# A graph layer on one core: 26 packed node ranges and 285 row gathers in place of 27 and 263

## The chip, the core and the metric

The kernel runs on one core of one Trainium2 chip. The metric is the device time of one execution in microseconds (us), given as the median of repeated runs. The engines are TensorE (PE; its weight loads are shown as PEld), VectorE (DVE), ScalarE (ACT), GpSimd (POOL) and SyncE (SP). Each engine works through its own queue in the order in which the program was written, so an instruction that waits holds up everything behind it on that engine.

## The reference

There are 6250 nodes with 128 features each and 100000 edges, sorted by their destination. Each edge has a type, 0 or 1, that selects one of two weight matrices. Cut to what matters:

```
Xs  = x[src]
msg = where(edge_type == 0, Xs @ W_data.T + b_data, Xs @ W_control.T + b_control)
agg = segment_sum(msg, dst)                       # 6250 x 128
h   = x + relu(agg + x @ W_self.T + b_self)
out = (h - mean(h)) / sqrt(var(h) + 1e-5)         # per row
```

## The kernel before, in words

**Messages first.** The product of every node with both weight matrices is made once: 12500 possible rows, held on the chip as `m3` (three bf16 parts of each float32 value, so a row has 384 columns) and also written to memory as `table`. This is the lead-in. PE multiplies (L490, L493, L501), ACT and DVE split the result into its parts (L436, L498, L505), and SP issues 13 writes of `table` (L509). After it, summing the messages of a destination is a matter of picking rows and adding them, and the kernel does this in two ways.

**Windows.** The first 27 x 160 = 4320 nodes are handled in 27 ranges of 160 nodes, called windows here. For each window a block of 21 x 128 edges is loaded (`win`). The function `ranks` sorts these edges into slots: it builds one-hot rows (`hots`, L691), counts on PE with triangular matrices how many edges of the same source block came before (L702; the weights are `every`, `tri` and `rest`), takes the count out with a DVE reduction (`slot`, L716), and scatters each edge's source and destination into a small packed list (L752). SP writes that list to memory (`packed`, L772 and L774). The few edges that find no slot are listed as well, and POOL fetches their rows with an indirect transfer (`sr`, L861). `ranks` works on several windows at once: the list `GROUPS` gives 1, 2 and then six times 4 windows. In the first two groups the 21 steps of the count are cut into chains of 6 and 12 steps (`CHAIN`), which run side by side in PSUM; a chain must first be told what the chains before it counted, and `add_to` with `every` does that.

The function `sums` then does one window after another. SP loads the packed list, broadcast to all partitions (`rows`, L904), DVE turns it into one-hot rows (L912), and PE multiplies 98 such blocks with `m3` (stage one, L933, four matmuls of 32 columns at a time). ACT or DVE moves each result out of PSUM (`gs`, L436), and PE multiplies it with a second one-hot matrix (`hot`, made on DVE at L920) into the window's sum `a` (stage two, L947 and L950).

**Gathers.** The last 1930 nodes are handled in blocks of 125 nodes by `gathered`. Per block 17 x 128 edges are loaded, and the last block, with 55 nodes, has 8 x 128. For each 128 edges POOL issues one indirect transfer that fetches 128 rows of `table` (`t_msg`, L1027, 14 buffers), DVE makes a one-hot matrix of destinations for up to six of them at once (`t_hot`, L1021), and PE adds the rows to the block's sum `ga` (L1034; the name has a single PSUM buffer). That makes 15 x 17 + 8 = 263 gathers. Together with the 14 fetches of `sr`, which stand in the same queue, POOL issues 277 such transfers.

`close` finishes windows and gathered blocks: it adds the parts, adds the residual, normalises, and writes `out` (L561 to L616).

**The order of the work.** Nothing is scheduled at run time. The class `Plan` collects all operations with an assumed duration, a due time and their dependencies, and simulates the engines once when the program is built; the order in which it starts operations is the order in which they are written into each engine's queue. A value `slack` on an operation holds it back by that much in the simulation, so that it is placed later in its queue; it adds no wait to the program. For the gathers the planner uses the duration `GC` and spaces their due times evenly:

```
    g0, g1 = T0 + G0, T0 + (NW + G1) * TW
    step = max((g1 - g0) / max(sum(GT), 20), GC + 0.02)
```

With `T0` = 36, `TW` = 13, 27 windows and 263 gathers the step is 1.32 in the planner's own units.

Of the kernel before, what the change touches and what calls it, by code (L numbers as in the profile page):

```python
# [16 lines left out]
SP = mybir.EngineType.SP  # L17
# [4 lines left out]
P = 128  # L22
# [16 lines left out]
WN = 160  # L39
KT = 21  # L40
WIN = KT * P
GROUPS = [1, 2] + [4] * 6
NW = sum(GROUPS)
R = 32
W4 = WN - P
# [46 lines left out]
class Plan:  # L92
# [10 lines left out]
    def add(self, engine, dur, fn, due, r=(), w=(), lat=0.0):  # L103
        alts = engine if isinstance(engine, list) else [(engine, dur, fn)]
        op = Op(alts, due, lat)
        op.index = len(self.ops)
        kind = [(i[0] if isinstance(i, tuple) else i).name for i in w] or ["out"]
        if engine == "SP" and due > self.FROM:
            op.slack = self.SLACK.get(kind[0], 0.0)
        self.ops.append(op)  # L110
        deps = set()
        for items, writes in ((r, False), (w, True)):
            for item in items:
                b, key = item if isinstance(item, tuple) else (item, None)
                for k, (ws, rs) in b.keys.items():
                    if key is None or k is None or k == key:
                        deps.update(ws)
                        if writes:
                            deps.update(rs)
                if writes and key is None:  # L120
                    b.keys = {}
                ws, rs = b.keys.setdefault(key, ([], []))
                if writes:
                    b.keys[key] = ([op], [])
                else:
                    rs.append(op)
                if not b.users or b.users[-1] is not op:
                    b.users.append(op)
        deps.discard(op)
        op.deps = list(deps)  # L130
        return op
# [95 lines left out]
@with_exitstack  # L227
def kernel(ctx, tc, x, xt, edges, w, bias, out):
    nc = tc.nc
    const = ctx.enter_context(tc.tile_pool(name="const", bufs=1))  # L230
    total = const.tile([1, 1], I32, name="total")

    with ExitStack() as main:
        sums_over_windows(main, tc, x, xt, edges, w, bias, out, total)

    matched = nc.values_load(total[0:1, 0:1])
    with tc.If(matched != E), ExitStack() as rest:
        sums_over_all(rest, tc, x, xt, edges, w, bias, out)
# [9 lines left out]
def sums_over_windows(ctx, tc, x, xt, edges, w, bias, out, total):  # L248
    nc = tc.nc
    V, A, G, T, S = nc.vector, nc.scalar, nc.gpsimd, nc.tensor, nc.sync  # L250
# [6 lines left out]
    add = plan.add  # L257

    table = dram.tile([NT * P, D3], BF16, name="table")
    packed = dram.tile([len(GROUPS), 2, P, NT], BF16, name="packed")  # L260

    def B(pool, shape, dtype, name, bufs=1, room=None):
        return Buf(plan, pool, shape, dtype, name, bufs, room)

    def C(shape, dtype, name):
        return Buf(plan, const, shape, dtype, name, 1)
# [3 lines left out]
    TW = 13.0  # L270
    LAT = 0.1
    G0, G1 = 0.0, -4
    GC = 1.3
    SPD = 0.45
    RP, RA, RS = 1, 14, 0.9

# [4 lines left out]
        lat=4.0)  # L281
# [15 lines left out]
    def vec(due, cols, fn, r, w, rate=1.04):  # L297
        return add("DVE", dve(cols, rate), fn, due, r, w)
# [44 lines left out]
    every = C([P, P], BF16, "every")  # L343
# [13 lines left out]
    for i in range(3):  # L357
        vec(0.3, P, lambda i=i: V.memset(one3.t[R * i : R * i + 1, :], 1.0), [], [one3], 0.3)
    counts = C([P, len(GROUPS) + NGB], F32, "counts")
    vec(2, 1, lambda: V.memset(counts.t, 0.0), [], [counts])  # L360
# [9 lines left out]
        op=ALU.is_gt), [r0f, bound_f], [begun])  # L370
    row_ps = low()

    def count_rows():
        for h in range(RH):
# [28 lines left out]
                                    start=True, stop=True), 0.8, [first_f, ident], [first_ps])  # L403
# [44 lines left out]
    packed_b = Buf(plan, None, None, None, "packed_b")  # L448
# [27 lines left out]
    for q in range(NS):  # L476
# [5 lines left out]
        n = 2 * nb * D  # L482
        ts = slice(4 * q, 4 * q + 2 * nb)

        for i, b in enumerate(bs):
            c, k, xk = pieces[b]
# [16 lines left out]
            skip_group_check=True), due + 1.2, [minus, (m3, (q, 0))], [mp])  # L503
# [117 lines left out]
    def ranks(gi, w0, nw, when, step, engines):  # L621
        nh = (nw + 1) // 2
        win = B(work, [P, nw, KT, 3], I32, "win", 2, 4 * KT * 3)
        for i in range(nw):
# [3 lines left out]
        n = nw * KT  # L628
# [19 lines left out]
                                                    op=ALU.arith_shift_right), [win], [cb])  # L648
        vec(when, n, lambda: V.tensor_single_scalar(wr(far), win.t[:, :, :, 2], 0.0,
                                                    op=ALU.not_equal), [win], [far])  # L650
# [5 lines left out]
                                                        op=ALU.bitwise_and), [win], [lo])  # L656
# [9 lines left out]
        L = CHAIN.get(gi, KT)  # L666
        nc_ = -(-KT // L)
# [11 lines left out]
        acc = B(ps, [P, 512], F32, "rk" if gi else "ga", 1)  # L679
# [4 lines left out]
        one = lambda k: hv(piece(k))[:, k - ks[piece(k)]]  # L684
        hkey = lambda k: (hots[piece(k)], (piece(k), (k - ks[piece(k)]) // 2))
        for ci in range(4):
            for k in range(ks[ci], ks[ci + 1], 2):
# [9 lines left out]
                        op=ALU.is_equal), [st1, iota1_b], [hkey(k)], 0.52)  # L697
        wide = nw * NT

        def add_to(c, wt, k, start, stop):  # L700
            for j in range(4):
                T.matmul(acc.t[R * j : R * j + R, c * wide : c * wide + wide],  # L702
                         wt.t[:, R * j : R * j + R], one(k).rearrange("p w c -> p (w c)"),
                         start=start, stop=stop, skip_group_check=True)
        mine = lambda r: [(c, c * L + r) for c in range(nc_) if c * L + r < min(KT, c * L + L)]
        for k in range((nc_ - 1) * L):
            add("PE", (nc_ - 1 - k // L) * wide / 2400, lambda k=k: [
                add_to(c, every, k, k == 0 and c == 1, False) for c in range(k // L + 1, nc_)], when + 1.5,
                [hkey(k), every], [acc])
        for r in range(L):  # L710
            due = when + 2 + step * r
            m = mine(r)
            add("PE", len(m) * wide / 2400, lambda r=r, m=m: [
                add_to(c, tri, k, r == 0 and nc_ == 1, k + 1 in (KT, c * L + L)) for c, k in m], due,
                [tri] + [hkey(k) for _, k in m], [acc])
            vec(due, len(m) * wide, lambda r=r, m=m: V.tensor_reduce(  # L716
                slot.t[:, r:KT:L, :],
                acc.t[:, : len(m) * wide].rearrange("p (k w c) -> p k w c", w=nw, c=NT),
                axis=AX.X, op=ALU.max), [acc], [(slot, r)]).lat = 2 * LAT
            m = [(c, k) for c, k in m if k + 1 < min(KT, c * L + L)]  # L720
            if m:
                add("PE", len(m) * wide / 2400, lambda m=m: [
                    add_to(c, rest, k, False, False) for c, k in m], due,
                    [rest] + [hkey(k) for _, k in m], [acc])
        base, slots = BASE, slot_f
        cs = {6: [0, KT], 12: [0, 12, KT]}.get(L, ks)
        for ci, (k0, k1) in enumerate(zip(cs, cs[1:])):
            dc = when + 3 + step * min(L, k1) + 0.5 * ci * (L < KT)
            m = (k1 - k0) * nw
            c = slice(k0 * nw, k1 * nw)  # L730
# [27 lines left out]
        d2 = when + 3.5 + step * L  # L758
        vs = B(work, [P, nh, NT], BF16, "vs", 1, 2 * NT)
# [10 lines left out]
        def put():  # L770
            if both:
                S.dma_start(packed[gi, :both].rearrange("h p c -> p h c"), vs.t[:, :both])  # L772
            if both < nh:
                S.dma_start(packed[gi, both, :64], vs.t[:64, both])  # L774
        add("SP", SPD, put, d2 + 1, [vs], [(packed_b, gi)], lat=2.0)
        to_d = B(work, [P, nw, NS, 2], BF16, "to_d", 2, 4 * NS * 2)
        for t in range(4):
            nx = NS if t < 2 else NS - 1
# [80 lines left out]
        for pr in range(nh):  # L859
            sr = B(work, [P, D3], BF16, "sr", 2)  # L860
            add("POOL", GC, lambda pr=pr, sr=sr: G.indirect_dma_start(  # L861
                out=sr.t[: room(pr)], out_offset=None, in_=table[:, :],
# [106 lines left out]
    def gathered(bis, when, step):  # L969

        nt, k_ = GT[bis[0]], len(bis)
        n = nt * k_
        gi = len(GROUPS) + bis[0]
        top = GB * max(GT)
# [32 lines left out]
        for j, bi in enumerate(bis):  # L1007
# [6 lines left out]
            for k in range(nt):  # L1014
                at = start + step * k
                kk = j * nt + k
                if k % KB == 0:
# [8 lines left out]
                m = B(work, [P, D3], BF16, "t_msg", 14)  # L1026
                add("POOL", GC, lambda m=m, kk=kk: G.indirect_dma_start(  # L1027
                    out=m.t, out_offset=None, in_=table[:, :],
# [16 lines left out]
    todo = []  # L1045
    for gi, nw in enumerate(GROUPS):
        if gi == 0:
            when, step, engines = 0.0, 0.9, ["SP"]
        elif gi == 1:
            when, step, engines = 8.0, 1.1, ["SP", "ACT"]  # L1050
        else:
            when, step, engines = T0 + w0 * TW - 58, 1.8, ["SP"]
            if gi == 2:
                when, step = 36.0, 1.3
        todo.append((gi, w0, nw, when, step, engines))
        w0 += nw
    placed = [ranks(*a) for a in todo]
    held = []
    for gi, w0, nw, *_ in todo:
# [4 lines left out]
        pairs = [(a, d) for _, a, d, _ in got]  # L1064
        if gi < len(GROUPS) - 1:
            close("", w0 * WN, WN, P, pairs, block, end)
# [3 lines left out]
    g0, g1 = T0 + G0, T0 + (NW + G1) * TW  # L1070
    step = max((g1 - g0) / max(sum(GT), 20), GC + 0.02)
    done = 0
# [154 lines left out]
```

## Time and profile before

| | us |
|---|---|
| median of 14 runs | 481.94 (476.54 to 487.32) |
| the profiled execution's own time | 482.76 |
| its span, from the first to the last instruction | 481.2 |
| PE busy | 443.8 |
| DVE busy | 395.0 |
| ACT busy | 354.3 |
| POOL busy | 301.3 |
| POOL, the 263 gathers of `t_msg` | 283.2, mean 1077 ns each |

The time of an execution is 1.6 us longer than its span, which is what lies around the instructions. Busy time is a share of the whole span: PE with 92% looks like the bound. An engine's queue can nevertheless be full with a lower share, when each of its instructions has a fixed pause before it that isn't counted as busy. A wait that is named in the profile is put down to the semaphore that came last.

### The profile page before, as it was taken

How to read it: one execution, taken by the hardware profiler on the slowest of the kernel's cores; microseconds unless marked ns; L12 is line 12 of the kernel's file. 1: busy time of each engine (PE TensorE's matmuls, PEld its weight loads, DVE VectorE, ACT ScalarE, POOL GpSimd, SP SyncE). 2: the span in 40 equal slices, each digit the busy share in tenths (PEclk: the TensorE clock that was granted, in tenths of full speed). 3: DMA queues.
4: the chain of work that ended last, by engine and by line, in shares of the span. 5: the costliest groups of instructions: out<-in, count | busy, mean ns of one | idle time of the engine just before them, and what ended most of it. 6: DMA issues, size and time to landing. Idle time of an engine off the chain costs nothing.

```text
span 481.2 us, 26926 instructions
## 1 busy us (share of the span) xinstructions
PE 443.8 (92%) x11461; PEld 362.2 (75%) x11461; DVE 395.0 (82%) x1271; ACT 354.3 (74%) x891; POOL 301.3 (63%) x290
## 2 busy tenths in 40 slices
PE   4999968997999889999999999999999999999990
PEld 3666656785888768788787878888889888878970
DVE  6799969998999969999888998888978779654343
ACT  2566764765877857778786788877888778989981
POOL 1100045777877777777777776777777757777700
PEclk9999998999999989999999999999999999999996
DMA  4589985438563546542765336764365524746210
GB/s 147 150 242 346 291 264 152 109 93 244 157 187 85 189 121 202 167 139 72 230 194 168 107 82 201 203 185 106 85 214 191 170 76 110 230 140 186 80 52 20
DMA packets 63117, 76.83 MB, mean 160 GB/s; under 512 B 21000, under 2 KB 52893, under 8 KB 62989
## 3 DMA queue, kind: packets, MB, share of 16 engines
q1 hardware_dynamic: 49147, 47.35, 31.3%
q0 software_dynamic: 13456, 27.42, 20.9%
q8 instruction: 91, 1.49, 1.2%
q10 hardware_dynamic: 386, 0.26, 0.2%
q14 instruction: 37, 0.30, 0.2%
HBM read 60.50 MB, written 13.17 MB: 153 GB/s over the span
## 4 chain that ended last, share of the span: by engine, by line
PE 74%; DVE 10%; DMA 7%; ACT 5%; issue 2%; SPq 0%; ACTq 0%; DVEq 0%
PE g L933 22%; PE a L947 20%; PE rk L702 9%; PE ga L1034 8%; PE a L950 3%; PE vt L752 3%; ACT gs L436 3%; DMA rows<-packed 2%; PE g L493 2%; DVE slot L716 2%; DMA t_msg<-table,t_idx 2%; DVE hot L920 1%; PE a L493 1%; ACT to_d L443 1%; PE a L518 1%
## 5 line engine op out<-in xcount | busy, mean ns | idle before, releaser
L1027 POOL DMA_INDIRECT t_msg<-table,t_idx x263 | 283.2, 1077 | 131.2 <-DVE hots L691 43.9
L436 ACT CAST gs<-g 128x384 bf16<-128x384 f32 x639 | 274.1, 481 | 79.4 <-PE g L933 63.2
L947 PE MATMUL a<-gs,hot 128*32 128x384 bf16 x2592 | 251.2, 331 | 7.9 <-ACT gs L436 5.3
L933 PE MATMUL g<-m,rows 128*32 128x384 bf16 x2646 | 255.6, 330 | 1.8 <-DVE rows L912 1.8
L933 PEld LDWEIGHTS <-rows 128*32 128x32 bf16 x2646 | 168.3, 135 | 13.9 <-DVE rows L912 2.1
L950 PE MATMUL a<-gs,hot 128*32 128x128 bf16 x1944 | 159.6, 220 | 0.4 <-issue 0.4
L947 PEld LDWEIGHTS <-hot 128*32 128x32 bf16 x2700 | 116.0, 95 | 35.2 <-issue 16.1
L1034 PE MATMUL ga<-t_msg,t_hot 128*32 128x384 bf16 x1036 | 102.2, 327 | 2.9 <-DMA t_msg<-table,t_idx 2.9
L716 DVE TENSOR_REDUCE slot<-rk 128x4 f32<-128x392 f32 (+1 forms) x138 | 76.5, 554 | 14.6 <-PE rk L702 9.0
L950 PEld LDWEIGHTS <-hot 128*32 128x32 bf16 x2025 | 81.8, 97 | 4.5 <-issue 0.7
L920 DVE TENSOR_TENSOR hot<-iota_b,to_d 128x1280 bf16<-128x1280 bf16 (+1 forms) x81 | 67.4, 842 | 0.0
L702 PE MATMUL rk<-hots,tri 128*32 128x392 bf16 (+1 forms) x588 | 61.2, 321 | 0.0
L702 PE MATMUL rk<-hots,rest 128*32 128x392 bf16 (+1 forms) x556 | 54.4, 321 | 5.0 <-DVE slot L716 4.8
L1034 PEld LDWEIGHTS <-t_hot 128*32 128x32 bf16 x1036 | 49.5, 97 | 6.9 <-issue 3.3
L912 DVE TENSOR_SCALAR rows<-rows,pid 128x1568 bf16<-128x1568 bf16 x54 | 36.0, 672 | 10.6 <-DMA rows<-packed 10.6
L691 DVE TENSOR_TENSOR hots<-iota_b,st 128x784 bf16<-128x784 bf16 (+1 forms) x83 | 39.2, 489 | 0.4 <-PE vt L752 0.2
L1021 DVE TENSOR_TENSOR t_hot<-iota_b,t_code 128x768 bf16<-128x768 bf16 (+2 forms) x47 | 24.6, 523 | 13.6 <-PE ga L1034 13.5
L702 PEld LDWEIGHTS <-rest 128*32 128x32 bf16 x624 | 24.7, 96 | 14.2 <-issue 11.6
L561 DVE TENSOR_REDUCE s<-a 128x128 f32<-128x384 f32 x27 | 15.0, 556 | 22.4 <-ACT bs L436 11.7
L702 PEld LDWEIGHTS <-tri 128*32 128x32 bf16 x672 | 28.6, 97 | 2.5
L752 PEld LDWEIGHTS <-two 128*64 128x64 bf16 x567 | 14.4, 109 | 8.5 <-DVE two L743 3.4
L861 POOL DMA_INDIRECT sr<-table,at x14 | 14.0, 1001 | 7.6 <-DVE at L849 3.5
(188 smaller groups left out, 528.6 us busy)
## 6 DMA issues: line engine op xcount, KB each, us to landing
rows<-packed SPq DMA_DIRECT2D x27, 784.0 KB
table<-m SPq DMA_DIRECT2D x12, 768.0 KB
t_msg<-table,t_idx POOLq DMA_INDIRECT x263
rows<-in_xt SPq DMA_DIRECT2D x8, 256.0 KB
xc<-in_xt SPq DMA_DIRECT2D x6, 320.0 KB
gl<-sr SPq DMA_DIRECT2D x27, 48.0 KB
xr<-in_x SPq DMA_DIRECT2D x5, 256.0 KB
out<-xr SPq DMA_DIRECT2D x5, 256.0 KB
```

The costliest lines, as they stand in the source:

```text
L436: [("ACT", act(cols), lambda: A.copy(o(), src())), ("DVE", dve(cols), lambda: V.tensor_copy(o(), src()))], None, None, due, r, w, lat)
L691: lambda k=k, kn=kn, ci=ci, hs4=hs4: V.tensor_tensor(hv(ci)[:, k - ks[ci] : k - ks[ci] + kn].rearrange("p k w (c d) -> p (k w) c d", d=2), ...
L702: T.matmul(acc.t[R * j : R * j + R, c * wide : c * wide + wide], wt.t[:, R * j : R * j + R], one(k).rearrange("p w c -> p (w c)"), start=s ...
L716: vec(due, len(m) * wide, lambda r=r, m=m: V.tensor_reduce(slot.t[:, r:KT:L, :], acc.t[:, : len(m) * wide].rearrange("p (k w c) -> p k w c ...
L752: T.matmul(vv()[q : q + 64, i // 2, :], two.t[:, (k - k0) * nw + i].rearrange("p f r -> p (f r)"), one(k)[:, i, :], start=k == 0 and i < 2 ...
L912: add("DVE", dve(half * NT, 0.335), lambda sp=sp, rs=rs: V.tensor_scalar(sp.t[:, rs], sp.t[:, rs], pid1.t, None, op0=ALU.is_equal), due - ...
L920: lambda i=i, hot2=hot2, s4=s4, c0=c0, c1=c1: V.tensor_tensor(hot2.t[:, c0:c1].rearrange("p g (c d) -> p g c d", d=2), iota1_b.t.rearrange ...
L933: T.matmul(gp.t[R * t : R * t + R, :D3], sp.t[:, :, 4 * g + t], m3.t[:, 4 * g + t, :], start=True, stop=True)
L947: T.matmul(a.t[R * j : R * j + R, :D3], hot2.t[:, g, R * j : R * j + R], gs.t, start=g == 0, stop=False, skip_group_check=True)
L950: T.matmul(a.t[R * c : R * c + R, D3:], hot2.t[:, g, P:], gs.t[:, c * D : (c + 1) * D], start=False, stop=last, skip_group_check=True)
L1027: add("POOL", GC, lambda m=m, kk=kk: G.indirect_dma_start(out=m.t, out_offset=None, in_=table[:, :], in_offset=bass.IndirectOffsetOnAxis(a ...
L1034: T.matmul(ga.t[R * i : R * i + R, :D3], hot.t[:, k % KB, R * i : R * i + R], m.t, start=k == 0, stop=False, skip_group_check=True)
```

## The change

Four edits:

- `GROUPS` ends in 3 windows instead of 4, so there are 26 windows. The last 2090 nodes are gathered: 16 blocks of 17 and one of 13, which is 285 gathers.
- `GC`, the planner's duration of a gather, is 1.26 instead of 1.3. The step of the due times becomes 1.28 (before 1.32).
- In `add_to`, one matmul writes the same counts into the places of several chains at once, by a broadcast operand, where there was one matmul for each. This concerns the first group alone, which has four chains: there are 72 matmuls and weight loads in place of 144, with the same number of streamed columns. The second group has two chains, and nothing changes in it.
- The write of `packed` of the second group gets a `slack` of 3.0, which moves it back in SP's queue.

```diff
-GROUPS = [1, 2] + [4] * 6
+GROUPS = [1, 2] + [4] * 5 + [3]
...
-    GC = 1.3
+    GC = 1.26
...
-        def add_to(c, wt, k, start, stop):
+        def add_to(c, wt, k, start, stop, n=1):
             for j in range(4):
-                T.matmul(acc.t[R * j : R * j + R, c * wide : c * wide + wide],
-                         wt.t[:, R * j : R * j + R], one(k).rearrange("p w c -> p (w c)"),
-                         start=start, stop=stop, skip_group_check=True)
+                T.matmul(acc.t[R * j : R * j + R, c * wide : (c + n) * wide].rearrange(
+                    "p (n c) -> p n c", n=n), wt.t[:, R * j : R * j + R],
+                    one(k).rearrange("p w c -> p (w c)")[:, None, :].to_broadcast([P, n, wide]),
+                    start=start, stop=stop, skip_group_check=True)
...
         for k in range((nc_ - 1) * L):
-            add("PE", (nc_ - 1 - k // L) * wide / 2400, lambda k=k: [
-                add_to(c, every, k, k == 0 and c == 1, False) for c in range(k // L + 1, nc_)], when + 1.5,
-                [hkey(k), every], [acc])
+            more = nc_ - 1 - k // L
+            add("PE", max(more * wide / 2400, 0.08), lambda k=k, more=more: add_to(
+                nc_ - more, every, k, k == 0, False, more), when + 1.5, [hkey(k), every], [acc])
...
-        add("SP", SPD, put, d2 + 1, [vs], [(packed_b, gi)], lat=2.0)
+        op = add("SP", SPD, put, d2 + 1, [vs], [(packed_b, gi)], lat=2.0)
+        if gi == 1:
+            op.slack = 3.0
```

As the planner sees the new numbers, every queue is written in a somewhat new order.

## The prediction

> **What bounds the kernel now.** I read the page first, then the gathers' tile, POOL's timeline, the same gathers by windows of time, and last the timelines of the end.
>
> ```profile
> PE 443.8 (92%) x11461; PEld 362.2 (75%) x11461; DVE 395.0 (82%) x1271; ACT 354.3 (74%) x891; POOL 301.3 (63%) x290
> ```
>
> By busy share PE is the bound and POOL has a third of its time free. The tile of the gathers and POOL's timeline say otherwise:
>
> ```profile
> L1027 POOL DMA_INDIRECT t_msg<-table,t_idx x263: 942/949/2419, 66.1 to 457.2; - x132
> ```
>
> ```profile
> 66.06 1.00 POOL L1027 DMA_INDIRECT t_msg<-table,t_idx  x1 [43.92 <-DVE hots L691]
> 67.37 0.97 POOL L1027 DMA_INDIRECT t_msg<-table,t_idx  x1 [0.30 <-issue]
> ...
> 76.66 1.12 POOL L1027 DMA_INDIRECT t_msg<-table,t_idx  x1 [0.30 <-issue]
> 81.23 1.03 POOL L861 DMA_INDIRECT sr<-table,at  x1 [3.46 <-DVE at L849]
> 82.57 0.95 POOL L1027 DMA_INDIRECT t_msg<-table,t_idx  x1 [0.30 <-issue]
> ...
> 288.13 0.94 POOL L1027 DMA_INDIRECT t_msg<-table,t_idx  x1 [0.30 <-PE g L933]
> 292.32 1.09 POOL L1027 DMA_INDIRECT t_msg<-table,t_idx  x1 [3.25 <-PE ga L1034]
> ...
> 390.44 0.94 POOL L1027 DMA_INDIRECT t_msg<-table,t_idx  x1 [0.30 <-PE rk L702]
> 394.87 1.61 POOL L1027 DMA_INDIRECT t_msg<-table,t_idx  x1 [3.49 <-PE ga L1034]
> ...
> 455.95 0.94 POOL L1027 DMA_INDIRECT t_msg<-table,t_idx  x1 [0.30 <-issue]
> 457.20 0.95 POOL L1027 DMA_INDIRECT t_msg<-table,t_idx  x1 [0.30 <-PE g L933]
> ```
>
> Before every gather POOL is idle for 0.30 us, whoever is named as releaser, so this is a fixed pause and no wait: the pitch is at least 0.95 + 0.30 = 1.25 us. From 66.06 to 457.20 POOL does nothing else, and only three pauses exceed 0.7 us: 3.46 for the row numbers `at`, and 3.25 and 3.49 where all 14 `t_msg` buffers were full. POOL's queue is therefore as full as PE's: of 391 us some 11 are free. Between 82.57 and 457.20 there are 266 steps (254 gathers, 12 fetches of `sr`); less 7.5 us of longer pauses that is 367.1 / 266 = 1.380 us each.
>
> ```profile
> 285.00:300.00 15.00, 7.34 (x7) 1.00 0.59 177
> 435.00:450.00 15.00, 11.65 (x12) 1.00 0.46 132
> 450.00:465.00 15.00, 6.32 (x7) 1.00 0.26 72
> ```
>
> These are the gathers alone by stretches (start and end, length, POOL's busy us and count, PE's granted clock, DMA share, GB/s): where DVE has little left (435 to 450: 7.5 of 15 us busy) twelve fit into 15 us, at 0.97 each against the mean of 1.077.
>
> **The change part by part.** *One window less* takes work from PE. Counting stage one in order of time, 98 matmuls to a window, the last windows, which have no `ranks` beside them, start at 432.3, 443.7 and 455.0: 11.4 us each. Earlier ones take 14 to 16, so a window's share of `ranks` is some 3.5. PE loses about 15 us. The window's `sr` fetch stays, since a group of 3 needs two, as a group of 4 does.
>
> *22 more gathers* cost PE little: four concurrent matmuls take 0.16 us in the chain, so 22 x 0.16 = 3.5, and PE alone would gain some 11. On POOL they cost 22 pitches, and there is nothing beside them. The changed order shows where: on PE 21 gathers stand behind the last window's last matmul, where before none did. DVE is nearly idle by then, so I take 1.26 each (450 to 458 shows 1.25, 438 to 457 1.28): 27.7 us. Bounds: 27.5 at the floor, 30.4 at the mean of 1.380.
>
> *The smaller `GC`* packs gathers denser in PE's order: gather 200 comes at window 19.7 (before 20.5), gather 136 at 13.7 (14.2). Their buffers come free earlier. The gather blocked until 394.87 waited for number 204's matmul at 394.1; that now stands at window 20.3, which PE reached at 380.1. So the two waits for buffers go, and a 0.7 at 214 with them: 2.9 + 3.2 + 0.7 = 6.8 us, between 0 and 6.8; I take 6.8, as the margin is 14 us. What is late next is the gather itself: PE then trails POOL by only the landing.
>
> *The merged matmuls* save 72 issues. 96 of the old ones were issued between 10.91 and 11.98, 11 ns each, and the columns streamed stay the same: at most 72 x 11 ns = 0.8 us, at least nothing. I take 0.3.
>
> *The moved write of `packed`.* SP stood at it from 58.80 to 61.40, waiting for `vs`, and the last write of `table` behind it went out at 62.80, though its data was ready at 61.8. Now that write goes first, and the first gather may start about 1.0 us earlier. Behind the moved write wait the `rows` broadcasts of windows 1 and 2, which go out some 2.5 us later.
>
> ```profile
> 70.88 0.63 DVE L912 TENSOR_SCALAR rows<-rows,pid 128x1568 bf16<-128x1568 bf16 x1 [3.23 <-DMA rows<-packed]
> ```
>
> DVE waited here for them, with `at` behind; the new order puts two pieces of `hot`, two of `hots` and two reductions (together 3.4 us) ahead. An earlier first gather only lengthens POOL's 3.46 us before 81.23: what counts is `at`. Rows 2.5 us later, 3.4 us of work moved into the wait and one reduction fewer before `at` give 1.2 us earlier; from 3.4 earlier (no pause left) to 2.5 later (the moved broadcasts alone).
>
> **The sum** for POOL's last gather: 82.57 - 1.2 + 367.1 (266 steps) + 0.6 (small pauses that stay) + 27.7 = 476.8 start, 477.7 end. Then its rows land: before, the completion mark came at 459.8, 1.7 after the last gather's end. PE needs 0.6 for the last matmuls:
>
> ```profile
> 463.93 0.34 PE L1034 MATMUL ga<-t_msg,t_hot 128*32 128x384 bf16 x2
> ...
> 464.32 0.23 PE L521 MATMUL ga<-brows,one 128*32 128x128 bf16 x2
> ```
>
> The block's closing takes from 469.33 to the write at 473.01, 3.7; from the issue of the last write to the span's end it was 5.9:
>
> ```profile
> 469.33 0.54 DVE L561 TENSOR_REDUCE s<-ga 55x128 f32<-55x384 f32 x1
> ```
>
> ```profile
> 473.01 0.31 SPq L612 DMA_DIRECT2D out<-xrg  x1
> ...
> 474.83 0.84 SPq L616 DMA_DIRECT2D out<-xr  x2
> ```
>
> With 0.1 for a hop this is 12.0, and the span 489.7. The profiled execution was 1.6 longer than its span (482.76 against 481.2) and lay 0.8 above the median of 481.94, so I expect 490.5 us, 1.8% slower. PE would have done its windows by about 455 and then follows POOL's pitch.
>
> [...] The granted clock was 0.91 in 60 to 75 us, where PE was busy for 11.2 of 15, and 1.00 nearly everywhere else. [...] Gathers that overlap a `hot` build (L920, a tensor-tensor operation) last 1.18 us in the mean, those that overlap none 1.03. [...]
>
> **The rivals.** *Faster, PE stays the bound.* For it speaks PE's 92% and that the two long waits were POOL's for PE. It needs a shorter pitch: the span equals today's if the last gather ends at 469.2, that is at a mean of (469.2 - 82.6) / 288 = 1.342 us. From 396.78 to 457.20 it was 60.4 / 45 = 1.343, so this is not absurd; but that stretch is in the mean already. If POOL reached window 26's end with all 14 buffers full, 7 gathers of the 21 would be left: 455 + 9 + 1 + 12 = 477, a time near 478.
>
> *No change.* `at` 3.4 earlier and a pitch of 1.36 on the 266 steps: 490.5 - 2.2 - 5.3 = 483.
>
> *Slower still.* The waits for buffers stay, since something else holds PE at those places: 490.5 + 6.8 = 497.3. Against it stands the margin of 14 us at number 204 (6 at 136).
>
> *The edit on the lead-in does nothing.* That is half of my forecast already: the 0.3 us and the earlier start vanish in the wait for `at`.
>
> **How the numbers follow.** The forecast, that POOL's queue ends last with the waits gone, gets 0.74; alone it spans 486 to 495 (`at` 2 each way, tail 1, pitch 0.01 each way). Slower still 0.14, no change 0.06, faster 0.06. The range from 483.5 to 498 takes in the forecast and the slower case. A measurement of this kernel tells 0.5% from no change: faster is below 479.5 (0.06), the same up to 484.4 (0.06), slower above (0.88).
>
> **What would show it.** In the changed profile: about 20 gathers with 0.30 us before each after the last stage-one matmul, PE waiting for `t_msg` there, the last gather near 477 and the last stage-one matmul near 455; no pause over 1 us on POOL after 85 us; `at` near 80. A last gather before 470 would prove the sum of pitches wrong; pauses of 3 us near 290 or 390, the part about the buffers.

## The result: 2.2% slower, and the profile after

| | before | changed |
|---|---|---|
| median, us | 482.58 (47 runs, 476.54 to 487.35) | 492.37 (10 runs, 487.07 to 494.99) |
| span of the profiled execution, us | 481.2 | 492.0 |
| last gather ends | 458.15 | 479.65 |
| last stage-one matmul ends | 467.5 | 457.5 |

The ratio is 1.0225, with a 95% interval from 1.0192 to 1.0258; here and below a ratio compares the fast executions of each kernel alone, those within 1.5% of its fastest, while the medians of all executions differ by 2.0%. PE did its windows 10 us sooner, and the execution ended 10.8 us later. The last matmuls of stage one, in the kernel before and in the changed one:

```profile
467.20 0.34 PE L933 MATMUL g<-m,rows 128*32 128x384 bf16 x2
```

```profile
457.14 0.35 PE L936 MATMUL g<-m,rows 128*32 128x384 bf16 x2
```

In the kernel before, no gather starts behind them; in the changed one 17 do. The page's line of busy times hides this again:

```profile
PE 440.9 (90%) x11178; PEld 356.7 (73%) x11178; DVE 390.3 (79%) x1275; ACT 343.7 (70%) x867; POOL 319.9 (65%) x312
```

PE still leads and POOL has a third of its time free. The tile of the gathers (count, then duration in ns as min/median/max, then first and last start) and POOL's timeline show the queue. `L1030` is the line that was L1027:

```profile
L1030 POOL DMA_INDIRECT t_msg<-table,t_idx x285: 942/947/2032, 68.6 to 478.7; - x143
```

```profile
68.62 1.01 POOL L1030 DMA_INDIRECT t_msg<-table,t_idx  x1 [45.87 <-DMA packed<-vs]
69.93 1.43 POOL L1030 DMA_INDIRECT t_msg<-table,t_idx  x1 [0.30 <-issue]
71.66 1.62 POOL L1030 DMA_INDIRECT t_msg<-table,t_idx  x1 [0.30 <-issue]
...
83.24 0.95 POOL L864 DMA_INDIRECT sr<-table,at  x1 [0.30 <-DVE slot L717]
...
387.09 0.95 POOL L1030 DMA_INDIRECT t_msg<-table,t_idx  x1 [1.44 <-PE rk L702]
389.27 1.13 POOL L1030 DMA_INDIRECT t_msg<-table,t_idx  x1 [1.24 <-PE ga L1037]
...
411.97 1.65 POOL L1030 DMA_INDIRECT t_msg<-table,t_idx  x1 [2.64 <-PE ga L1037]
...
477.45 0.95 POOL L1030 DMA_INDIRECT t_msg<-table,t_idx  x1 [0.30 <-issue]
478.70 0.95 POOL L1030 DMA_INDIRECT t_msg<-table,t_idx  x1 [0.30 <-issue]
```

From 68.62 to 479.65 there is no gap of more than half a microsecond but the three pauses shown, of 1.24 to 2.64 us: POOL is the queue that ends last. The pause of 3.25 us near 290 is gone. Of the one of 3.49 us near 390, two of 1.44 and 1.24 us are left, and the one at 412 is new. The first gather starts 2.56 us later than before, not earlier. The gathers alone by stretches (POOL's busy us and count, then PE's granted clock) end like this:

```profile
435.00:450.00 15.00, 11.65 (x12) 1.00 0.31 86
450.00:465.00 15.00, 11.34 (x13) 0.93 0.37 100
465.00:480.00 15.00, 11.29 (x12) 0.50 0.34 96
```

At the end twelve fit into 15 us, a pitch of 1.25, while PE, which has little left but the gathers' matmuls, is granted a clock of 0.50. In PE's list of waits (total us, times, longest) the gathers' rows went from 2.9 us in one wait to:

```profile
PE ga L1037 <- DMA t_msg<-table,t_idx: 17.4, 16, 3.2
```

The end itself, from the timelines of PE, DVE and SP:

```profile
481.29 0.51 PE L1037 MATMUL ga<-t_msg,t_hot 128*32 128x384 bf16 x3 [0.75 <-DMA t_msg<-table,t_idx]
```

```profile
482.37 0.55 DVE L561 TENSOR_REDUCE s<-ga 90x128 f32<-90x384 f32 x1 [6.53 <-PE ga L521]
```

```profile
485.62 0.34 SPq L612 DMA_DIRECT2D out<-xrg  x1
```

Landing 1.64, PE 1.08, closing 3.25, and 6.40 from the issue of the last write to the end: 12.37 us behind the last gather.

### The profile page after: what moved, and what is told of

Same layout as the page of the kernel before. It is cut to its first block, busy times and chain, and to the rows that moved or that the text cites. A ratio compares the mean times of both kernels' runs of the same rounds, so it can differ in the third digit from the quotient of the medians.

```text
span 492.0 us, 26354 instructions
## 1 busy us (share of the span) xinstructions
PE 440.9 (90%) x11178; PEld 356.7 (73%) x11178; DVE 390.3 (79%) x1275; ACT 343.7 (70%) x867; POOL 319.9 (65%) x312
## 3 DMA queue, kind: packets, MB, share of 16 engines
q0 software_dynamic: 14496, 29.53, 21.9%
## 4 chain that ended last, share of the span: by engine, by line
PE 68%; DMA 13%; DVE 6%; ACT 5%; issue 4%; POOL 1%; POOLq 0%; SPq 0%; ACTq 0%
PE g L936 19%; PE a L950 18%; DMA t_msg<-table,t_idx 9%; PE ga L1037 8%; PE rk L702 8%; PE a L953 3%; PE vt L753 3%; ACT gs L436 2%; PE g L493 2%; ACT to_d L443 1%; POOL t_msg L1030 1%; PE a L493 1%; DMA sr<-table,at 1%; DMA win<-in_edges 1%; PE a L518 1%
## 5 line engine op out<-in xcount | busy, mean ns | idle before, releaser
L1030 POOL DMA_INDIRECT t_msg<-table,t_idx x285 | 300.8, 1055 | 136.8 <-DMA packed<-vs 45.9
L436 ACT CAST gs<-g 128x384 bf16<-128x384 f32 x614 | 263.7, 481 | 75.1 <-PE g L936 56.5
L936 PE MATMUL g<-m,rows 128*32 128x384 bf16 x2548 | 244.1, 328 | 1.7 <-issue 1.7
L950 PE MATMUL a<-gs,hot 128*32 128x384 bf16 x2496 | 240.3, 329 | 5.9 <-ACT gs L436 3.8
L1037 PE MATMUL ga<-t_msg,t_hot 128*32 128x384 bf16 x1127 | 113.6, 335 | 19.3 <-DMA t_msg<-table,t_idx 17.4
L717 DVE TENSOR_REDUCE slot<-rk 128x4 f32<-128x392 f32 (+2 forms) x138 | 74.7, 541 | 25.8 <-PE rk L702 17.4
L923 DVE TENSOR_TENSOR hot<-iota_b,to_d 128x1280 bf16<-128x1280 bf16 (+1 forms) x78 | 65.1, 840 | 0.0
L702 PE MATMUL rk<-hots,tri 128*32 128x392 bf16 (+2 forms) x588 | 58.3, 311 | 0.0
L702 PE MATMUL rk<-hots,rest 128*32 128x392 bf16 (+2 forms) x556 | 54.5, 314 | 2.6 <-DVE slot L717 2.6
L691 DVE TENSOR_TENSOR hots<-iota_b,st 128x784 bf16<-128x784 bf16 (+3 forms) x83 | 38.1, 475 | 0.4 <-PE vt L753 0.4
L561 DVE TENSOR_REDUCE s<-a 128x128 f32<-128x384 f32 x26 | 14.4, 556 | 20.3 <-ACT bs L436 16.7
L753 PE MATMUL vt<-hots,two 128*64 128x98 bf16 x525 | 17.1, 209 | 1.0 <-issue 0.8
```

Of the source, the lines that this page charges most:

```text
L436: [("ACT", act(cols), lambda: A.copy(o(), src())), ("DVE", dve(cols), lambda: V.tensor_copy(o(), src()))], None, None, due, r, w, lat)
L691: lambda k=k, kn=kn, ci=ci, hs4=hs4: V.tensor_tensor(hv(ci)[:, k - ks[ci] : k - ks[ci] + kn].rearrange("p k w (c d) -> p (k w) c d", d=2), ...
L702: T.matmul(acc.t[R * j : R * j + R, c * wide : (c + n) * wide].rearrange("p (n c) -> p n c", n=n), wt.t[:, R * j : R * j + R], one(k).rear ...
L717: vec(due, len(m) * wide, lambda r=r, m=m: V.tensor_reduce(slot.t[:, r:KT:L, :], acc.t[:, : len(m) * wide].rearrange("p (k w c) -> p k w c ...
L753: T.matmul(vv()[q : q + 64, i // 2, :], two.t[:, (k - k0) * nw + i].rearrange("p f r -> p (f r)"), one(k)[:, i, :], start=k == 0 and i < 2 ...
L923: lambda i=i, hot2=hot2, s4=s4, c0=c0, c1=c1: V.tensor_tensor(hot2.t[:, c0:c1].rearrange("p g (c d) -> p g c d", d=2), iota1_b.t.rearrange ...
```

## The experiments

The theory is that POOL's queue of gathers ends last, so that 22 more of them cost their pitch (the time from the start of one to the start of the next). The main rival is the lead-in: the first gather came 2.6 us late, and the small edits or the new order could have made a good part of the loss. Every median below stands beside the median of the kernel before in the same series, from 481.9 to 483.4.

### Taking the last 22 gathers away again

In the changed kernel POOL issues no gather for the last 22 blocks of edges; their matmuls stay and use older rows.

```diff
+                if issued[0] < sum(GT) - 22:
+                    m = B(work, [P, D3], BF16, "t_msg", 14)
...
+                    issued.append(m)
+                else:
+                    m = issued[-1]
+                issued[0] += 1
```

> The changed kernel without its last 22 gathers on POOL: their matmuls stay and use the rows of an earlier gather, so the last 2 blocks' sums are left wrong and only POOL's and the landing's work is taken out. Theory A (POOL's queue sets the end): the last gather ends 22 x 1.25 = 27.5 us earlier than 479.65, near 452; the last stage-one matmul stays near 457.5, the 22 gathers' matmuls add at most 3.5, and closing and last write 9.6, so the span is near 471 and the time 473 within 3. Theory B (PE or the landing of rows sets it): 488 or more.

Measured: 475.71 us, ratio to the kernel before 0.986 (0.978 to 0.994), 16.7 below the changed kernel.

```profile
L1031 POOL DMA_INDIRECT t_msg<-table,t_idx x263: 940/948/2035, 66.9 to 449.0; - x132
```

The last gather ends at 449.9, PE finishes stage one at 456.6 and the last gathered matmul at 462.9, and the span is 473.5. So the gathers were the bound, by 16.7 us over PE. The sums of the last blocks are left wrong by this edit. Of the 27.5 us taken off POOL, the rest is where PE takes over.

### The same 22 taken from the kernel before

The same edit in the kernel with 27 windows.

> The kernel before without its last 22 gathers on POOL, their matmuls kept in the same way (the sums of the last blocks are left wrong). Theory A (at 27 windows PE's windows set the end, and POOL's queue, though full, does not): time 482 within 2, last stage-one matmul near 467. Theory B (POOL sets the end before as well): 476 or less.

Measured: 483.86, ratio 1.0045 (1.0001 to 1.0089).

```profile
L1028 POOL DMA_INDIRECT t_msg<-table,t_idx x241: 942/968/2036, 68.1 to 427.1; - x121
```

The last gather now ends near 428 instead of 458, the last stage-one matmul at 466.7, and nothing is gained. At 27 windows PE's windows set the end, and POOL's queue, though nearly full, has room. The two runs together show a crossing: PE ends last with 27 windows, POOL with 26.

### One window less again

```diff
-GROUPS = [1, 2] + [4] * 5 + [3]
+GROUPS = [1, 2] + [4] * 5 + [2]
```

> The changed kernel with one window less again: GROUPS ends in 2, 25 windows, 306 gathers, 13 fetches of sr instead of 14. Theory A (POOL's queue sets the end, and each further gather costs its pitch): 21 x 1.25 to 1.35 less 1.25 for the fetch, 25 to 27 us on top, time 517 to 520; the last stage-one matmul near 446; the 41 or so gathers behind it at 1.25 each. Theory B (the loss of the change was mostly lead-in and waits, not the count): below 507.

Measured: 518.14, ratio 1.0739 (1.0676 to 1.0802). That is 25.8 us over the changed kernel, for 21 gathers more and one fetch of `sr` less: 1.29 us for each of the 20, or 1.19 by the ends of the last gathers in the two profiles (503.47 and 479.65). The last stage-one matmul ends at 444.5, and 47 transfers start behind it. The price of a window is now the pitch of its gathers, as near as these runs can tell.

### Each edit alone

The window count alone (the first of the four edits):

> The kernel before with 26 windows and 285 gathers alone (GC 1.3, separate matmuls, the write where it was). Theory A (22 more gathers in POOL's queue make the loss): 491 to 496, with the pauses for buffers perhaps still there; 26 windows alone also move the second write of table ahead of window loads on SP, so DVE waits over 1 us for a load of win near 23 us and the first gather starts at 67.5 or later. Theory B (merged matmuls and moved write make a third of the loss): 488 to 489.

Measured: 493.68, ratio 1.029 (1.016 to 1.042): the whole loss, without the other three. The last gather ends at 478.2. DVE did not wait for `win`, against the expectation, and the pauses for buffers near 290 and 390 shrank to 1.5 and 2.0 with GC still at 1.3.

The moved write alone:

> The kernel before with the moved write of packed alone. Theory A (as predicted): the last write of table goes out about 1 us earlier than 62.80, the first gather starts near 65.0, and POOL's wait for at grows or stays, so the time is 482 within 1.5. Theory B (the write of table lands when the writes before it have drained, whenever it is issued): the last write goes out near 61.8 and still lands at 65.2 or later, the first gather starts at 66.0 or later; time 482.6 to 484.

Measured: 483.84, ratio 1.0033 (0.9989 to 1.0076): no effect. In its profile the first gather starts at 65.11, as predicted. One profile does not show that the edit did this, as in the six other kernels with separate matmuls it starts anywhere from 65.96 to 68.22.

GC 1.26 alone:

> The kernel before with GC 1.26 alone. Both theories: the pauses for buffers near 288 and 390 us (2.9 and 3.2) go and the last gather ends 6 to 7 us earlier, near 451.5. Theory A (at 27 windows PE's windows set the end): time 480 to 483. Theory B (POOL already set the end before): 475.8.

Measured: 486.56, ratio 1.0088 (1.0047 to 1.0128), slower than either theory said. The pauses for buffers near 290 and 390 go, others of 1.4 and 3.4 us come at 338 and 414, and the last gather ends at 454.8, but PE waits for rows more often, and its last stage-one matmul ends at 472.5 instead of 467.5. From PE's list of waits:

```profile
PE ga L1034 <- DMA t_msg<-table,t_idx: 5.8, 5, 2.9
```

GC 1.34, the other way:

> The kernel before with GC 1.34 alone (step 1.36, near the measured mean pitch of 1.38). Theory A (a GC below the true pitch puts the gathers' matmuls on PE ahead of their rows, and PE's windows wait behind them; 1.26 cost 0.9%): PE waits less for t_msg than 2.9 us, the windows end earlier than 467.5, time 480 to 483, while the buffers stay full longer and POOL's last gather ends at 460 or later. Theory B (POOL's later gathers become the end): 486 or more.

Measured: 488.61, ratio 1.0116 (1.0071 to 1.0162). PE waits 4.0 us for rows, not less than 2.9, and stage one ends at 469.8. So the theory that a GC below the true pitch is what costs falls: both directions lose about 1% at 27 windows. Theory B had the number right, and its reason in part. The last gathered block now ends behind the windows, at 473.6, but POOL is not late: its last gather ended at 464.1. The block's matmuls wait for `ga`, its one PSUM buffer, which DVE empties at 472.1:

```profile
472.15 1.48 PE L1034 MATMUL ga<-t_msg,t_hot 128*32 128x384 bf16 x16 [0.37 <-DVE s L561]
```

What the two directions share is that every queue is written anew.

The merged matmuls alone, in two series:

> The kernel before with the merged matmuls alone (27 windows, GC 1.3, no moved write). After, the 72 merged matmuls and their neighbours of the first group took from 10.78 to 12.57 us where 144 took from 10.91 to 11.95 before. Theory A (the merging itself is slower, 0.22 us for a group of four with 294 columns against 3 x 0.045): the stretch again lasts about 1.8 us, first gather 0.7 us later than before, time 483.3. Theory B (PE ran at half pace until some moment of the execution that has nothing to do with the edit): the pace doubles at a moment that differs from both runs (10.9 and 12.5 us), after which a merged group of four costs no more than 0.13 us; time 482.6 within 1.

> The kernel before with the merged matmuls alone, again, in more executions (e1_merge had 4, from 480.7 to 490.8, and no verdict). Theory A (merging delays the lead-in through the fetch beside the load of win and PE's windows pass it on): 484 to 486. Theory B (no effect at 27 windows): 482.6 within 1. The fetch of instructions again between 21 and 22 us, with DVE's wait of 1 us or more for win.

Measured: the first gave four executions from 480.72 to 490.77, too few and too far apart for a ratio; the second 487.66 in 12 executions, ratio 1.0101 (1.0059 to 1.0143), more than both theories. The first window starts at 57.2 instead of 55.5, so the lead-in is longer; but the kernels are level at window 12 (256.7 and 257.3), and the last 5 us are lost between windows 14 and 24 (437.1 against 432.3 at window 24), where the order of the queues differs. What does it there was not separated.

### Why the lead-in got longer

DVE waits 1.39 us for the load of `win` in the changed kernel. The first suspect was SP's order: with 26 windows the second write of `table` stands ahead of two of these loads. One hold puts it back:

```diff
+            if q == 3:
+                op.slack = 1.5
```

> The changed kernel with one hold of 1.5 on the second write of table, so that SP issues the loads of win before it, as in the kernel before. Theory A (the lead-in's delay passes to the end through POOL's full queue): DVE's wait of 1.4 us for win near 23 us goes, the first gather starts near 67.2 and the last ends 1.4 us earlier, time near 491. Theory B (the later waits take the gain back): 492.4 within 0.7.

Measured: 490.68, ratio to the kernel before 1.015 (1.007 to 1.023); DVE's wait of 1.4 us stays. The order is not the cause, and the 1.7 us against the changed kernel lie within the spread of its executions.

The profiles gave another suspect, the fetch of instructions. The changed kernel with separate matmuls tests it:

> The changed kernel with the separate matmuls of before. In the profiles so far the four kernels with merged matmuls have an instruction fetch of 16 KB between 21.1 and 21.9 us, beside the load of win that is under way, and DVE waits 1.0 to 1.4 us for that load; the six with separate matmuls have the fetch at 22.7 to 24.7 and no such wait. Theory A (the merged form moves the fetch into the load): here the fetch is at 22.5 or later and DVE waits less than 0.3 us, while the time stays 492.4 within 1.5, since POOL's later steps differ more than this. Theory B (the wait comes from SP's order with 26 windows): the wait of 1 us or more is there again.

Measured: 493.69, ratio 1.0241 (1.0179 to 1.0303), and no wait for `win`. DVE's timeline of the changed kernel first, then of this one:

```profile
24.61 0.21 DVE L639 TENSOR_TENSOR rel<-win,wbase 128x42 f32<-128x42 int32 x1 [1.39 <-DMA win<-in_edges]
```

```profile
23.26 0.20 DVE L639 TENSOR_TENSOR rel<-win,wbase 128x42 f32<-128x42 int32 x1
```

In all seven kernels with merged matmuls a 16 KB packet of the instruction queue starts between 20.8 and 21.9 us, while the 252-byte packets of the load of `win` that ACT issued are under way; their last one starts at 23.4 to 24.0, and DVE waits 1.0 to 1.7 us. In the seven with separate matmuls the packet comes at 22.7 to 24.7, and the load's last packet had started by 22.7. With 72 matmuls and as many weight loads fewer in the queue, the fetch comes earlier and meets the load. That the fetch holds the load up is read from these times; no run moved the fetch alone.

This kernel also says what an earlier start is worth. Its tenth transfer starts at 78.95, 4.3 us before that of the changed kernel, yet its last gather ends at 479.95, 0.3 us later. Most of it goes at the first fetch of `sr` for the third group, the 35th transfer, which needs row numbers `at` as well:

```profile
115.62 0.94 POOL L863 DMA_INDIRECT sr<-table,at  x1 [3.58 <-DVE at L851]
```

In the run with the hold on `table` the tenth transfer started 2.9 us early, and POOL waited 1.65 us at the same fetch. Six of the 14 profiles have such a wait there, of 1.5 to 4.8 us. In the changed kernel POOL came to it at 116.32, with `at` ready since 114.97 and so without a wait. The main rival, the late first gather, is held by this to little more than 1 us of the loss, as long as `at` comes when it does.

### Do DVE's builds lengthen the gathers?

In the changed kernel `hot` is built for the first window only and used for all.

```diff
+                if w0 + i:
+                    break
```

> The changed kernel with the one-hot matrix hot built for the first window only and used for all windows (the windows' sums are left wrong; 25 x 3 tensor-tensor builds leave DVE). 76 of 299 gathers overlapped such a build and lasted 1.211 us in the mean, the others 1.001. Theory A (the overlap with tensor-tensor work lengthens the gathers): the mean falls from 1.056 to 1.00 or 1.02, the last gather ends 10 to 16 us earlier than 479.65, time 477 to 483. Theory B (the longer gathers only coincide with it): mean 1.04 to 1.06, time 490 or more.

Measured: 503.32, ratio 1.0423 (1.0345 to 1.0502). The mean of the 299 transfers fell from 1.056 to 1.003 us, as theory A says, which is 16 us of POOL's time. Yet it got slower: POOL's long pauses grew from 4.4 to 31.4 us, 3.8 of them for `at` and nearly all the others because PE fell behind and the 14 buffers filled. PE's largest wait is:

```profile
PE rk L702 <- DVE slot L717: 14.4, 12, 3.2
```

It was 2.6 us in the changed kernel. With less work on DVE the planner wrote another order, in which the counting of `ranks` waits on its reductions. The lengthening by DVE is shown; what it would be worth in an unchanged order is not.

None of these kernels beats the kernel before in a complete computation.

## Why the prediction was right, step by step

The cause was right: POOL's queue ends last, PE has its windows done before it and follows the gathers' pitch, and the moved write alone buys nothing. The sum was 489.7 for the span against 492.0 measured, and it came this close because errors cancel:

- **The start, +3.1.** The step behind the tenth transfer was set at 82.57 - 1.2 = 81.4 and came at 84.50. This step failed: it took `at` for what counts. The tenth transfer, a fetch of `sr`, waited for nothing but the gathers before it, and these were late (68.62) and slow (1.43 and 1.62 us). Two terms were to make it earlier. The merged matmuls were to give 0.3 us; the first window starts at 56.9 to 58.6 us in all seven kernels that have them and at 55.4 to 56.2 in the seven that have not. How much of this reaches the first gather is open, which starts at 66.6 to 68.6 in the former and at 65.1 to 68.2 in the latter. The 11 ns per issue that were counted as saved are no cost: where PE runs at full pace, a merged group of four with 196 columns takes 0.088 us and two separate groups 2 x 0.043. And the moved write made the first gather earlier when alone (65.11), but here the last write of `table`, issued at 63.86, had its last packets at 67.2; the two large writes before it had gone out 2.3 us later. A single profile fixes such a start badly: the tenth transfer starts between 78.6 and 83.2 in the 14 profiles. The sum also counts the start in full and leaves out the second wait for `at` near 115 us. An earlier start would have gained about 1 of these 3.1 us and waited the rest there.
- **The pitch, -5.0.** 288 steps less the long pauses took 389.8 us against 394.8. The tail's part was right: the last 22 steps took 1.27 each, the last twelve 1.25, where 1.26 was taken. The 266 steps before took 1.361 instead of 1.380.
- **Long pauses, +3.8.** All waits for buffers were to go. Those at 214 and 290 did; of the 3.2 us near 390, 2.1 stayed (387 and 389), and 2.3 at 412 are new. That is 4.4 us against 0.6, without the fixed 0.30 of each step. So 3.0 us were regained: inside the term's bounds of 0 to 6.8, but not at the end that was taken. This step failed because it looked at one matmul. Number 204 did stand at window 20.3 and started at 381.58, near the 380.1 of the prediction. Numbers 205 and 206 stand behind it at windows 20.5 and 20.6 and started at 386.42 and 388.42, and the next two gathers waited for their buffers. The credit given to `GC` was wrong too: the window count alone leaves 3.3 us of the pauses, `GC` alone 4.2 at 27 windows, and the two together 4.4. The new pause, of gather 235 for matmul 221, stands in all seven kernels with `GC` 1.26 and in no other. The prediction did not see where such pauses fall. The three that were to go waited for matmuls 85, 136 and 204, the new one for 221: 5, 8, 12 and 13 times 17, each the first matmul of a block, which needs the one buffer of `ga`. No run tests a second buffer.
- **The tail, +0.4.** 12.37 against 12.0. PE's part was 1.08 instead of 0.6, closing 3.25 instead of 3.7, the write 6.40 instead of 5.9. The 0.1 for a hop was the author's estimate, and no run shows it apart; DVE's first closing step starts at 482.37, 0.04 us behind the end of PE's last matmuls.

These make +2.3 for the span; the median lies 0.35 above the profiled span instead of 0.8, and 490.5 + 2.3 - 0.45 gives the 492.4 measured.

Of the rivals, "PE stays the bound" was priced at 478 and would have needed a mean pitch of 1.342. Reckoned in the same way, with all pauses, it was (479.65 - 84.50) / 288 = 1.372, and 1.354 without the long pauses. The 475.7 us without the 22 gathers show that PE's part of that rival was nearly right and its pitch was not. "Slower still" needed buffers' waits of 7 us. "The edit on the lead-in does nothing" was half of the forecast; it did harm there, and in the changed kernel none that the time shows, as the later wait for `at` takes up most of the difference: with and without merging it is 492.4 and 493.7.

The prediction also gives two measured rows that bear on the tail, the granted clock and the `hot` builds. PE's clock was 0.50 from 463 us on, and its last matmuls took 1.08 us; in the kernel before it was 1.00 at 464, and they took 0.6. The tail's last 22 steps took 1.27 us each and not the mean of 1.380, while DVE was busy for 6.04 us of 450 to 465 and for 3.54 us of 465 to 480. Without the `hot` builds the mean transfer was 0.053 us shorter; no run shows which part of a transfer they lengthen.

## What to carry to other kernels

An engine whose every instruction has a fixed pause before it, 0.30 us on POOL here, can be the bound at 65% busy; count its steps by pitch, and set the last step against the other engines' last work. Where two queues are both nearly full, moving work from one to the other pays only up to their crossing, here less than one window. Time gained ahead of a wait can be lost at the next one, as most of 4.3 us was here at a wait of 3.58 us for `at`: find the last wait in a queue before adding up what stands ahead of it. When a planner writes the order, a small edit has two effects, its own and that of the new order: three edits here that promised nothing or a gain cost about 1% each. That the new order makes this loss is the likeliest reading; no run kept the order and changed the edit alone.

## What the runs showed of the hardware that was not expected

- PE starts at half pace and doubles it at a moment that does not go with the edits. In the first group a set of four 98-column matmuls takes 0.081 us and then 0.043; the change falls at 10.8 us in the profile of before, at 12.5 in the changed kernel, and between 10.7 and 12.9 in all 14, with merged and separate matmuls alike. All stretches of the clock records but the last are multiples of 3.41 us (46, 1 and 85 of them in the changed kernel).
- The profile's clock column shows 1.00 for that first stretch, although the pace is half: the trace's clock record only begins at the doubling.
- Single windows of 3.41 us at clock 0.50 also occur in the middle, none to three in a profile (169.5 us in the changed kernel, 72.2 and 171.2 before). The windows ahead of them are not idle: PE was busy for 1.09 of the 3.41 us ahead of 169.5, and for 0.70 and 1.06 ahead of 72.2 and 171.2. In the 14 profiles every fall to 0.50 follows a window with 1.85 us or less, and every full-pace window with more is followed by 1.00. So the window ahead of a fall need not be idle.
- The queue that the profile lists as `q8 instruction` moves 16 KB packets (91 of them, 1.49 MB, in the kernel before), which are read here as fetches of instructions; the one near 20 to 25 us lasted 0.9 to 2.0 us among the data's packets. Where it met the load of `win`, that load's last packet started at 23.4 to 24.0 us, elsewhere at 22.0 to 22.7.
